# Re-spacing the key stage of a delta-rule block in a hand-interleaved decoder kernel

## The chip, the core and the metric

The kernel is one program on one core of one Trainium2 chip, written in Bass with the Tile framework. The metric is device microseconds of an execution, the median of three runs. All arithmetic is float32.

## What is computed

The reference is a decoder layer on a batch of 4 sequences of 512 tokens, width 512: a delta-rule attention (16 heads of 128 channels), then a quantised cross-attention, then softmax attention with a mixture of experts. The change touches only the first block:

```python
q = causal_conv(x @ Wq.T)   # 4 taps and silu; k and v alike
g = exp(-exp(A_log) * softplus(x @ Wa.T + dt_bias)); beta = sigmoid(x @ Wb.T)
q, k = l2norm(q), l2norm(k)                 # per head
for each token t:                           # state S: 128 x 128 per head
    error = v_t - g_t * (S^T k_t)
    S = g_t * S + k_t (beta_t * error)^T
    o_t = S^T q_t
out = (rmsnorm(o) * silu(x @ Wg.T)) @ Wo.T
```

## The kernel before, in words

**Pairs.** The recurrence is worked in chunks of 128 tokens, four per sequence. Work is cut into 32 pairs of heads (4 sequences times 8 pairs, `NP` = 32), and one pass of the main loop (line 993) handles pair m. Inside a chunk the recurrence becomes a triangular system whose inverse is needed for each of the pair's 8 head-chunks.

**Streams.** Each part is a Python generator that emits some instructions and yields. While `stage3(m)` (line 751, the recurrence itself, 15 yields) is emitted for pair m, the other streams are emitted between its yields. One round between two yields is called a turn here, T1 to T15. In a turn, in this order: one step of `output(m - 1)` (line 871, the product with Wo), two steps of `stage1(m + 2)` (line 552, keys and queries), one step of `stage2_values(m + 1)` (line 718, values and gates), and two steps of `inversions(m, turn)` (line 703).

**Who orders the engines.** The order on VectorE (DVE), ScalarE (ACT) and GpSimd (POOL) is the emission order, as line 977 asks. TensorE (PE) and the DMA queue of SyncE (SP) are not in that list: the framework's planner orders them from its own costs, so a PE instruction may be placed ahead of its place in the emission.

**stage1, in steps.** A `conv` (line 527) has four steps for keys and queries: half the projection (line 533), the other half with an ACT scaling (line 541), two of three DVE taps (line 544), the last tap with the silu (line 547). Steps 1 to 4 are the key of head 0, steps 5 to 8 that of head 1. Step 9 loads a table row (line 560) and the next weights, then turns the key of head 0 to tokens: four PE transposes (line 576), an ACT copy (line 578), four ACT squares that sum into `ss` (line 581). Step 10 does the same for head 1. Step 11 computes `rk`, `ee`, `ke`, `nr` from `ss` (lines 587 to 592: one on DVE, five on POOL) and scans the decay table `em` of head 0 on DVE (line 597), step 12 that of head 1. Steps 13 and 14, one per head, scale `em` by `ee` on ACT (line 402, four instructions), form key-by-key products on PE (line 606), combine both on DVE to `at` (line 609) and store it (line 610). Step 15 begins with `load_blocks` (line 668), which loads `at` back in the shape of the inversion (lines 672 and 673). Then follow the two query convs, the products (line 621), the decayed keys (line 402 again), and the sums of squares (line 652), to step 26. With two steps per turn, step 2k ends turn k.

**Inverses.** `stage2_inverse` (line 676) has 33 pieces: 31 elimination steps of two tensor operations each (lines 684 and 685), one with a copy and two stores (lines 690 to 692), one with the two loads (lines 697 and 698). Inverses of even pairs run on DVE, of odd pairs on POOL. In the pass of pair m, the inverse of m + 1 is finished and that of m + 2 begun, so a pass with even m finishes a POOL inverse while a pass with odd m finishes a DVE one. `inversions` takes one or two pieces per step, in turn; one turn is three pieces. The new inverse begins in the turn after next once `load_blocks` was emitted (`loaded > 4`), at one piece per step.

**stage3, by its yields.** Segments 1 to 4 join the inverse's quarters on PE and ACT (lines 765 to 799). Then, per chunk c: `r` (for c > 0: PE line 817, DVE line 819), `u` (PE line 826, ACT copy line 828), and the new state and outputs (PE lines 836, 844, 846; state on ACT line 839 or DVE line 841). Chunk 0 takes segments 5 and 6, chunk 1 segments 7 to 9, chunk 2 segments 10 to 12, chunk 3 segments 13 to 15.

**PSUM.** All of `pj`, `tp`, `pk`, `pw` and the like come from one pool of four buffers, `p_b` (line 342); the recurrence has its own.

**Start and end.** Before the loop, pairs 0 and 1 are prepared together with the cross-attention's keys and values (`prepare`, line 917, whose transposes of quantised keys are line 953). In the pass of pair 30 there is no `stage1`.

Of the kernel before, what the change touches and what calls it, by code (L numbers as in the profile page):

```python
# [31 lines left out]
F32 = mybir.dt.float32  # L32
AF = mybir.ActivationFunctionType
ALU = mybir.AluOpType
# [4 lines left out]
P = 128  # L39
B, S, D = 4, 512, 512  # L40
# [5 lines left out]
HG = 2  # L46
# [52 lines left out]
def decoder(ctx: ExitStack, tc: tile.TileContext, a: dict, out: bass.AP):  # L99
# [73 lines left out]
    def run(*gs):  # L173
        for g in gs:
            for _ in g:
                pass
# [154 lines left out]
    with ExitStack() as st:  # L331
# [64 lines left out]
        def chunks(t):  # L396
            return t.rearrange("p c j -> p (c j)")
# [121 lines left out]
        def load_weights(m, *what, by=nc.sync):  # L519

            for n in what:
                if m < B * NHG:
                    t = (s1 if n < 2 else s2).tile([P, KD, HG * P], F32, name=f"w{n}", bufs=1)
                    by.dma_start(t, a["a_w"][m % NHG][:, n])
                    weights[m, n] = t
# [26 lines left out]
        def stage1(m):  # L552

            b, hg = divmod(m, NHG)
            hh = slice(hg * HG, (hg + 1) * HG)
            wk, wq = weights.pop((m, 1)), weights.pop((m, 0))

            def rows(n):
                t = s1.tile([P, HG, S], F32, name=f"row{n}", bufs=1)
                nc.sync.dma_start(chunks(t), g_d[b, n, hg * HG * TB : (hg + 1) * HG * TB].rearrange("c t -> (c t)").partition_broadcast(P))  # L560
                return [t[:, p, :] for p in range(HG)]

            kT, kt = [], []
            ss = small.tile([P, HG * TB], F32, name="ss", bufs=2)
            for p in range(HG):
                t = live.tile([P, S], F32, name="kT")
                yield from conv(b, hg, p, 1, wk, t)
                kT.append(t)
                yield
            xnT, beta, gam, ngam, gend, gall = seqs[b]  # L570
            gb = rows(0)
            load_weights(m + 1, 1)
            for p in range(HG):
                tp = p_b.tile([P, TB, P], F32, name="pb")
                for c in range(TB):
                    nc.tensor.transpose(tp[:, c, :], kT[p][:, c * P : (c + 1) * P], ident)
                t = s1.tile([P, TB, P], F32, name="ktok")
                nc.scalar.copy(t, tp)
                kt.append(t)
                for c in range(TB):  # L580
                    nc.scalar.activation(tp[:, c, :], tp[:, c, :], AF.Square, accum_out=ss[:, p * TB + c : p * TB + c + 1])
                yield

            rk, ee, ke = (small.tile([P, HG * TB], F32, name=n, bufs=2) for n in ("rk", "ee", "ke"))
            nr = small.tile([P, HG * TB], F32, name="nr", bufs=4)
            flat = lambda t: t[:, hh, :].rearrange("p h c -> p (h c)")
            nc.vector.tensor_scalar(ss, ss, 1e-24, None, ALU.max)  # L587
            nc.gpsimd.tensor_tensor(rk, ss, mhalf[:, 0 : HG * TB], ALU.pow)  # L588
            nc.gpsimd.tensor_tensor(ee, rk, rk, ALU.mult)
            nc.gpsimd.tensor_tensor(ee, ee, flat(beta), ALU.mult)  # L590
            nc.gpsimd.tensor_tensor(ke, ee, flat(gend), ALU.mult)
            nc.gpsimd.tensor_tensor(nr, ss, rk, ALU.mult)
            em = []
            for p in range(HG):

                e = s1.tile([P, TB, P], F32, name="em")
                nc.vector.tensor_tensor_scan(chunks(e), gb[p], id4, 0.0, ALU.mult, ALU.add)
                em.append(e)
                yield
            ats = []  # L600
            for p in range(HG):
                scale(em[p], em[p], ee, p)
                pk = p_b.tile([P, TB, P], F32, name="pb")
                for c in range(TB):
                    k_ = kT[p][:, c * P : (c + 1) * P]
                    nc.tensor.matmul(pk[:, c, :], k_, k_, start=True, stop=True)
                at = live.tile([P, TB, P], F32, name="at", bufs=4)
                ats.append(at)
                nc.vector.scalar_tensor_tensor(at, pk, -1.0, em[p], ALU.mult, ALU.mult)
                nc.sync.dma_start(squares(at_d[m % SLOTS][p * TB : (p + 1) * TB]), at)  # L610
                yield
            load_blocks(m, ats)
            mb = rows(1)

            qh, qg, pt, sq, kd_ = [], [], [], [], []

            def product(p):
                pq = p_b.tile([P, TB, P], F32, name="pb")
                for c in range(TB):
                    cs = slice(c * P, (c + 1) * P)  # L620
                    nc.tensor.matmul(pq[:, c, :], kT[p][:, cs], qh[p][:, cs], start=True, stop=True)
                t = live.tile([P, TB, P], F32, name="pt", bufs=6)
                nc.vector.tensor_tensor(t, pq, em[p], ALU.mult)
                pt.append(t)

            def decayed(p):
                t = live.tile([P, TB, P], F32, name="kdec", bufs=4)
                scale(t, kt[p], ke, p)
                kd_.append(t)

            for p in range(HG):
                q = s1.tile([P, S], F32, name="qh")
                c = conv(b, hg, p, 0, wq, q)
                yield from itertools.islice(c, 2)
                if p:
                    product(0)
                yield from c
                qh.append(q)
                g = live.tile([P, S], F32, name="qg", bufs=6)
                nc.gpsimd.tensor_tensor(g, q, mb[p], ALU.mult)  # L640
                qg.append(g)
                t = w2.tile([P, S], F32, name="cv", bufs=5)
                nc.scalar.activation(t, q, AF.Square)
                sq.append(t)
                yield
            load_weights(m + 1, 0)
            decayed(0)
            yield

            pss = p_b.tile([P, S], F32, name="pb")  # L650
            for p in range(HG):
                nc.tensor.matmul(pss[p * 32 : (p + 1) * 32, :], tab_a[:, C_ONE, 0:32], sq[p], start=True, stop=True)
            sr = small.tile([P, S], F32, name="sr", bufs=1)
            nc.scalar.copy(sr[0 : 32 * HG], pss[0 : 32 * HG])

            rq = small.tile([P, HG * TB], F32, name="rq", bufs=2)
            for p in range(HG):
                nc.sync.dma_start(rq[p * P // HG : (p + 1) * P // HG, :], sr[p * 32 : p * 32 + 1, :].rearrange("o (n k) -> o n k", k=HG * TB))
            yield
            product(1)  # L660
            yield
            decayed(1)
            yield
            keys[m] = (kT, kd_, qg, pt, nr, rq)
# [38 lines left out]
        def inversions(m, turn):  # L703


            n, loaded, left = 0, 0, True
            while left or turn:

                for _ in range(1 + n % 2):
                    left = left and next(begun[m + 1], None) is not None  # L710
                n += 1
                loaded += m + 2 in inverses
                if turn and loaded > 4:
                    next(begun.setdefault(m + 2, stage2_inverse(m + 2)), None)
                yield
            begun.setdefault(m + 2, stage2_inverse(m + 2))
# [200 lines left out]
        def prepare():  # L917
# [24 lines left out]
            for kt in range(2):  # L942
                pk = p_b.tile([P, D], F32, name="pb")
                for kd in range(KD):
                    nc.tensor.matmul(pk, ctxT[kt][:, kd, :], wk[kd], start=kd == 0, stop=kd == KD - 1)
                k = temp()
                nc.vector.tensor_tensor(k, pk, bk, ALU.add)
                yield
                quantised(k, k, H2, HD2, small)
                yield  # L950
                tp = p_b.tile([P, KD, P], F32, name="pb")
                for kd in range(KD):
                    nc.tensor.transpose(tp[:, kd, :], k[:, kd * P : (kd + 1) * P], ident)
                t = temp()
                nc.scalar.copy(t, chunks(tp))
                yield
                nc.sync.dma_start(x_kT_d[:, :, kt * P : (kt + 1) * P], t.rearrange("p (c k) -> p c k", c=KD))
# [29 lines left out]
        pair0 = stage1(0)  # L987
        run(turns((start, 1), (itertools.islice(pair0, 2 * HG * 2), 1)))

        run(itertools.islice(pair0, 3 * HG + 1))  # L990
        run(turns((stage2_inverse(0), 2), (chain(pair0, turns((stage1(1), 2), (stage2_values(0), 1))), 1), (prepare(), 1)))
        begun[1] = stage2_inverse(1)
        for m in range(NP):
# [609 lines left out]
```

## Time and profile before

| what | us |
|---|---|
| median of 3 runs (3775.2 to 3777.73) | 3776.95 |
| the profiled execution | 3771.82 |
| its span, first to last instruction | 3769.0 |
| delta-rule passes in it (142 to 1962) | 1820.0, PE busy 1688.33 |
| its start (0 to 142) | 142.0, PE busy 95.87 |
| last pass and turn-over (1962 to 2150) | 188.0, PE busy 147.87 |
| the rest (2150 to 3769) | 1619.0, PE busy 1506.41 |
| PE granted clock, whole span | 0.961 |

A pass is told by the start of its first matmul of line 765. Busy times are unions of instruction times; matmul ends are modelled, so a gap between two rows is read from the bracket behind a timeline row (idle time before it, and what ended it), not from start plus duration. A float32 matmul of 512 columns is recorded as two instructions of 592 ns at full clock, so the half of a projection is a row "x4".

### The profile page before, as it was taken

The page shows a single profiled execution, that of the slowest core. Times are in us where ns is not written, and L with a number is a line of the kernel's source. Part 1 is how long each engine was busy: PE and PEld are TensorE (multiplying, and loading weights), DVE is VectorE, ACT ScalarE, POOL GpSimd, SP SyncE. Part 2 cuts the span into 40 slices and gives each one's busy share as a digit, 9 for nine tenths or more (in the row PEclk, how much of TensorE's full clock was granted, in tenths as well). Part 3 has the DMA queues.
Part 4 walks back from the last instruction along what each step waited for, and adds up shares of the span by engine and source line. Part 5 has one row for each costly group of instructions (what it writes and reads, how often), then busy time and mean ns, then how long its engine had stood idle before and what let it go on. Part 6 is the DMA issues. An engine that isn't in the chain of part 4 may idle for free. (4 is left out here: it accounts for less than half of the span.)

```text
span 3769.0 us, 48754 instructions
## 1 busy us (share of the span) xinstructions
PE 3438.5 (91%) x16466; PEld 1916.5 (51%) x16466; DVE 2208.8 (59%) x4923; ACT 1583.5 (42%) x4379; POOL 1378.5 (37%) x1941
## 2 busy tenths in 40 slices
PE   5889999999899999999997789999999999898897
PEld 3545555555555555555554455555555555554443
DVE  5667666775677666765674455656655655554111
ACT  3444444444444444444442243444544444343121
POOL 1544555346543564455543222213112111211442
PEclk7999999999999999999998799999999999999998
DMA  5334333433334342434341435445444544446444
GB/s 157 108 100 124 101 108 95 146 100 114 96 107 139 95 123 83 121 115 118 97 126 37 168 132 168 139 137 159 148 137 135 162 143 134 149 151 209 87 84 92
DMA packets 391879, 465.54 MB, mean 124 GB/s; under 512 B 128451, under 2 KB 242115, under 8 KB 391440
## 3 DMA queue, kind: packets, MB, share of 16 engines
q1 hardware_dynamic: 380080, 438.03, 37.7%
q0 software_dynamic: 10112, 21.58, 3.0%
q8 instruction: 131, 2.15, 0.2%
q10 hardware_dynamic: 1440, 2.84, 0.2%
q14 instruction: 116, 0.95, 0.1%
HBM read 401.76 MB, written 64.81 MB: 124 GB/s over the span
## 5 line engine op out<-in xcount | busy, mean ns | idle before, releaser
L533 PE MATMUL pb<-xnT,w 128*128 128x512 f32 x2048 | 974.5, 611 | 18.7 <-issue 9.9
L533 PEld LDWEIGHTS pb<-xnT,w 128*128 128x128 f32 x2048 | 374.4, 195 | 417.7 <-issue 399.8
L544 DVE SCALAR_TENSOR_TENSOR cv<-pb,pp,cv 128x510 f32<-128x510 f32 (+2 forms) x576 | 423.6, 744 | 29.9 <-ACT cv L541 17.6
L1145 PE MATMUL pb<-c_q,hT 128*128 128x512 f32 x768 | 358.2, 605 | 9.7 <-DMA c_q<-in_c_wq_dram 3.3
L685 POOL TENSOR_TENSOR iT<-iT,iW 32x31 f32<-32x31 f32 (+15 forms) x496 | 275.2, 555 | 38.9
L684 POOL TENSOR_TENSOR iW<-iA,iT 32x31 f32<-32x31 f32 (+15 forms) x496 | 249.1, 502 | 56.0 <-DMA iA<-at_d 13.7
L890 PE MATMUL pb<-wot,og 128*128 128x512 f32 x512 | 250.9, 613 | 2.0 <-issue 1.5
L1251 PE MATMUL pw<-c_o,oT 128*128 128x512 f32 x512 | 241.5, 602 | 2.9 <-DVE oT L1243 2.9
L1145 PEld LDWEIGHTS pb<-c_q,hT 128*128 128x128 f32 x768 | 142.7, 194 | 165.7 <-issue 152.8
L1217 ACT ACTIVATE e<-pb,nm,rq 128x128 f32<-128x128 f32 (+3 forms) x256 | 157.0, 618 | 143.8 <-DVE nm L1215 111.3
L685 DVE TENSOR_TENSOR iT<-iT,iW 32x31 f32<-32x31 f32 (+15 forms) x496 | 206.9, 417 | 17.1
L640 POOL TENSOR_TENSOR qg<-qh,row 128x512 f32<-128x512 f32 x64 | 82.6, 1291 | 358.7 <-ACT qh L547 311.2
L541 ACT ACTIVATE cv<-pb,pp 128x512 f32<-128x512 f32 x192 | 148.6, 774 | 153.4 <-PE pb L533 150.2
L684 DVE TENSOR_TENSOR iW<-iA,iT 32x31 f32<-32x31 f32 (+15 forms) x496 | 186.1, 375 | 45.8 <-DMA iA<-at_d 35.2
L895 DVE TENSOR_TENSOR xa<-pb,xa 128x512 f32<-128x512 f32 x112 | 76.9, 687 | 198.4 <-PE pb L890 198.4
L588 POOL TENSOR_TENSOR rk<-ss,mhalf 128x8 f32<-128x8 f32 x32 | 66.8, 2086 | 343.9 <-DVE ss L587 343.0
L279 POOL TENSOR_SCALAR x_e<-x_e 128x1024 f32<-128x1024 f32 x64 | 67.4, 1054 | 332.1 <-ACT x_e L274 235.5
L1241 PE MATMUL po<-eT,val 128*128 128x512 f32 x320 | 170.6, 626 | 6.9 <-ACT eT L1239 3.8
L274 ACT ACTIVATE x_e<-pb,nm 128x256 f32<-128x256 f32 x256 | 118.2, 476 | 111.7 <-DVE nm L271 105.8
L1211 PE MATMUL pb<-kT,qT 128*128 128x256 f32 (+3 forms) x576 | 162.7, 409 | 0.8 <-ACT x_e L274 0.8
L1073 POOL TENSOR_TENSOR rope_s<-q,tab 128x128 f32<-128x128 f32 x64 | 34.8, 544 | 315.8 <-DVE q L1175 269.9
L547 ACT ACTIVATE qh<-cv 128x512 f32<-128x512 f32 x64 | 40.3, 630 | 251.9 <-DVE cv L544 239.6
(330 smaller groups left out, 6596.1 us busy)
## 6 DMA issues: line engine op xcount, KB each, us to landing
c_o<-in_c_wo_dram SPq DMA_DIRECT2D x128, 512.0 KB, 4.0
c_q<-in_c_wq_dram SPq DMA_DIRECT2D x128, 512.0 KB, 4.6
w<-in_a_w_dram SPq DMA_DIRECT2D x124, 512.0 KB, 4.0
row<-g_d SPq DMA_DIRECT2D x64, 512.0 KB, 3.7
at_d<-at SPq DMA_DIRECT2D x64, 256.0 KB, 2.7
T<-t_d SPq DMA_DIRECT2D x32, 512.0 KB, 4.1
X<-x_d SPq DMA_DIRECT2D x32, 512.0 KB, 5.3
rrow<-r_d SPq DMA_DIRECT2D x32, 512.0 KB, 3.6
```

What stands on the lines that cost most here:

```text
L274: nc.scalar.activation(e[:, n, :], ps[r][:, g, :], AF.Exp, bias=nm[:, n : n + 1], accum_out=ssum[:, n : n + 1])
L533: nc.tensor.matmul(pj, wt[:, kd, p * P : (p + 1) * P], xnT[:, kd, :], start=kd == 0, stop=kd == KD - 1)
L541: nc.scalar.activation(ac, pj, AF.Identity, bias=cb[:, m, h : h + 1], scale=cw[:, m, h, 3:4])
L544: nc.vector.scalar_tensor_tensor(ac[:, j:], pj[:, : S - j], cw[:, m, h, 3 - j : 4 - j], ac[:, j:], ALU.mult, ALU.add)
L684: eng.tensor_tensor(u, A[:, i, i + 1 :].unsqueeze(2).to_broadcast([nb, n, w]), T[:, i, :w].unsqueeze(1).to_broadcast([nb, n, w]), ALU.mult)
L685: eng.tensor_tensor(T[:, i + 1 :, :w], T[:, i + 1 :, :w], u, ALU.add)
L890: nc.tensor.matmul(pw, og[p][:, c * P : (c + 1) * P], wot[:, p, :], start=p == 0, stop=p == HG - 1)
L1145: nc.tensor.matmul(pj, hT[:, kd, :], w[:, kd % 2, :], start=kd == 0, stop=kd == KD - 1)
L1211: nc.tensor.matmul(ps[:, m, k * P : (k + w) * P], qT[g][:, n + m, :], kT[:, g, j : j + w, :], start=True, stop=True)
L1217: nc.scalar.activation(e[n + m][:, :nk], ps[:, m, :nk], AF.Exp, bias=nm[:, n + m : n + m + 1], scale=rq, accum_out=es[:, n + m : n + m + 1])
L1241: nc.tensor.matmul(po, val[:, g, :], eT, start=k == 0, stop=k == c)
L1251: nc.tensor.matmul(pw, oT[:, h + m, :], w[:, m, :], start=g == 0 and h + m == 0, stop=g == 3 and h + m == 3)
```

## The change

In `stage1`, the key of head 0 is turned to tokens (and squared) inside the conv of head 1, after its second step (step 7), that of head 1 in step 10. The first `em` scan moves to step 9, the second to step 11. The table row is loaded at the start of `stage1`, except for pair 0. A step with nothing in it follows the second scan, and another lies between the two heads' scalings, so that these are steps 13 and 15, in turns T7 and T8; `load_blocks` and the first half of the query projection are step 16, and `stage1` ends with step 27. In `inversions`, one step in four takes two pieces, the others one (five pieces in two turns), and in the pass of pair 30 every step takes two. `prepare` yields once more between quantising a key tile and transposing it. No instruction is added or removed.

```diff
--- before.py
+++ after.py
@@ -560,17 +560,12 @@
                 nc.sync.dma_start(chunks(t), g_d[b, n, hg * HG * TB : (hg + 1) * HG * TB].rearrange("c t -> (c t)").partition_broadcast(P))
                 return [t[:, p, :] for p in range(HG)]
 
-            kT, kt = [], []
+            kT, kt, em, ats = [], [], [], []
             ss = small.tile([P, HG * TB], F32, name="ss", bufs=2)
-            for p in range(HG):
-                t = live.tile([P, S], F32, name="kT")
-                yield from conv(b, hg, p, 1, wk, t)
-                kT.append(t)
-                yield
-            xnT, beta, gam, ngam, gend, gall = seqs[b]
-            gb = rows(0)
-            load_weights(m + 1, 1)
-            for p in range(HG):
+            xnT, beta, gam, ngam, gend, gall = seqs[b] if m else seqs[b] + [None] * 5
+            gb = rows(0) if m else None
+
+            def by_token(p):
                 tp = p_b.tile([P, TB, P], F32, name="pb")
                 for c in range(TB):
                     nc.tensor.transpose(tp[:, c, :], kT[p][:, c * P : (c + 1) * P], ident)
@@ -579,7 +574,30 @@
                 kt.append(t)
                 for c in range(TB):
                     nc.scalar.activation(tp[:, c, :], tp[:, c, :], AF.Square, accum_out=ss[:, p * TB + c : p * TB + c + 1])
-                yield
+
+            def decays(p):
+
+                e = s1.tile([P, TB, P], F32, name="em")
+                nc.vector.tensor_tensor_scan(chunks(e), gb[p], id4, 0.0, ALU.mult, ALU.add)
+                em.append(e)
+
+            for p in range(HG):
+                t = live.tile([P, S], F32, name="kT")
+                c = conv(b, hg, p, 1, wk, t)
+                yield from itertools.islice(c, 2)
+                if p:
+                    by_token(0)
+                yield from c
+                kT.append(t)
+                yield
+            load_weights(m + 1, 1)
+            if m == 0:
+                xnT, beta, gam, ngam, gend, gall = seqs[b]
+                gb = rows(0)
+            decays(0)
+            yield
+            by_token(1)
+            yield
 
             rk, ee, ke = (small.tile([P, HG * TB], F32, name=n, bufs=2) for n in ("rk", "ee", "ke"))
             nr = small.tile([P, HG * TB], F32, name="nr", bufs=4)
@@ -590,14 +608,9 @@
             nc.gpsimd.tensor_tensor(ee, ee, flat(beta), ALU.mult)
             nc.gpsimd.tensor_tensor(ke, ee, flat(gend), ALU.mult)
             nc.gpsimd.tensor_tensor(nr, ss, rk, ALU.mult)
-            em = []
-            for p in range(HG):
-
-                e = s1.tile([P, TB, P], F32, name="em")
-                nc.vector.tensor_tensor_scan(chunks(e), gb[p], id4, 0.0, ALU.mult, ALU.add)
-                em.append(e)
-                yield
-            ats = []
+            decays(1)
+            yield
+            yield
             for p in range(HG):
                 scale(em[p], em[p], ee, p)
                 pk = p_b.tile([P, TB, P], F32, name="pb")
@@ -609,6 +622,8 @@
                 nc.vector.scalar_tensor_tensor(at, pk, -1.0, em[p], ALU.mult, ALU.mult)
                 nc.sync.dma_start(squares(at_d[m % SLOTS][p * TB : (p + 1) * TB]), at)
                 yield
+                if p == 0:
+                    yield
             load_blocks(m, ats)
             mb = rows(1)
 
@@ -706,7 +721,7 @@
             n, loaded, left = 0, 0, True
             while left or turn:
 
-                for _ in range(1 + n % 2):
+                for _ in range(1 + (n % 4 == 1 or m == NP - 2)):
                     left = left and next(begun[m + 1], None) is not None
                 n += 1
                 loaded += m + 2 in inverses
@@ -948,6 +963,7 @@
                 yield
                 quantised(k, k, H2, HD2, small)
                 yield
+                yield
                 tp = p_b.tile([P, KD, P], F32, name="pb")
                 for kd in range(KD):
                     nc.tensor.transpose(tp[:, kd, :], k[:, kd * P : (kd + 1) * P], ident)
@@ -987,7 +1003,7 @@
         pair0 = stage1(0)
         run(turns((start, 1), (itertools.islice(pair0, 2 * HG * 2), 1)))
 
-        run(itertools.islice(pair0, 3 * HG + 1))
+        run(itertools.islice(pair0, 8))
         run(turns((stage2_inverse(0), 2), (chain(pair0, turns((stage1(1), 2), (stage2_values(0), 1))), 1), (prepare(), 1)))
         begun[1] = stage2_inverse(1)
         for m in range(NP):
```

## The prediction

> **What bounds the kernel now.** I read the page first, then PE's waits over the delta-rule passes, then the timelines of one even and one odd pass, then the clock by windows.
>
> ```profile
> PE 3438.5 (91%) x16466; PEld 1916.5 (51%) x16466; DVE 2208.8 (59%) x4923; ACT 1583.5 (42%) x4379; POOL 1378.5 (37%) x1941
> ```
>
> PE is the bound, the others have slack, so only PE's idle time and its clock can be won. In the passes (142 to 1962) PE is busy 1688.33 of 1820.0 us: 131.7 us of idle in 30 passes. The view of PE's waits in that window says who ends it:
>
> ```profile
> PE pb L576 <- ACT kT L547: 38.2, 30, 2.3
> PE ps L836 <- ACT u L828: 23.3, 11, 2.6
> PE ps L826 <- DVE r L819: 14.5, 12, 1.4
> PE pb L533 <- issue: 9.9, 3, 3.3
> PE pb L621 <- ACT qh L547: 8.6, 7, 2.4
> PE ps L817 <- ACT state L839: 7.6, 26, 0.4
> ```
>
> (Columns: total us, times, longest.) The first is in every pass, nearly always 1.13 us. L836 and L621 stand in passes with even m, L826 in odd ones. Pass 14 (even), the timelines of all engines, shows how two of them arise:
>
> ```profile
> 1012.70 1.98 PE L890 MATMUL pb<-wot,og 128*128 128x512 f32 x4
> ...
> 1018.41 0.66 PE L576 MATMUL pb<-tab,kT 128*128 128x128 f32 x4 [1.13 <-ACT kT L547]
> 1023.72 1.43 POOL L684 TENSOR_TENSOR iW<-iA,iT 32x156 f32<-32x156 f32 x1
> 1023.69 2.54 DVE L597 TENSOR_TENSOR_SCAN em<-row,tab_a 128x512 f32<-128x512 f32 x2
> 1027.60 1.64 POOL L588 TENSOR_TENSOR rk<-ss,mhalf 128x8 f32<-128x8 f32 x1
> 1029.83 2.44 ACT L402 ACTIVATE em<-em,ee 128x128 f32<-128x128 f32 x8 [5.92 <-POOL ee L590]
> 1032.84 0.41 ACT L828 COPY u<-ps 128x128 f32<-128x128 f32 x2
> 1033.14 0.71 PE L836 MATMUL ps<-u,kdec 128*128 128x128 f32 x4 [2.37 <-ACT u L828]
> ```
>
> PE's 2.37 us are not the recurrence's own latency: its `u` copy stands on ACT behind eight scalings that wait 5.92 us for `ee`, which waits on POOL behind inverse pieces. In the odd pass 15, three pieces, both scans and three more pieces stand ahead of `r` on DVE (1081.57 to 1088.46), and line 826 waits 1.39 us. The clock, by windows:
>
> ```profile
> 1016.90:1020.30 3.40, 2.27 (x20) 1.85 (x19) 2.59 (x4) 2.52 (x7) 3.01 (x6) 1.00 0.00 0
> 1030.90:1034.30 3.40, 1.16 (x10) 1.16 (x11) 2.60 (x4) 3.02 (x9) 2.86 (x8) 1.00 0.50 113
> 1034.34:1037.75 3.41, 3.41 (x11) 2.18 (x10) 3.34 (x7) 0.33 (x1) 2.29 (x2) 0.50 1.04 255
> ```
>
> (PEclk is third from the end.) The 1.13 us gap leaves it at 1.00; the 2.37 us gap is followed by one 3.41 us window at 0.50.
>
> **The change, part by part.** No instruction comes or goes; all that moves is who stands behind whom.
>
> *Keys to tokens.* PE's position at the second key's transposes stays the same: between line 890's third product (1012.70) and line 576 at step 10 lie four transposes, 0.6 us, before and after, only in another place. The chain that ends the wait is unchanged too: DVE's add of that product, three taps at 744 ns, silu 0.63, ending 18.36 (times from 1000). So I book nothing for the largest wait. Its bounds: all 38.2 us, if the planner pulls a later projection in front; or a loss, costed as a rival. The copy and four squares of key 0 (0.60 + 4 x 0.40 = 2.2 us of ACT) now stand ahead of key 1's silu: transposes end near 15.1, ACT is through at 17.4, the taps end at 17.6. Hidden by 0.2 us; if not, those tenths go to the wait.
>
> *`ss` sooner, fewer pieces ahead of `ee`.* In T5 ACT turns one key, not two: `ss` is complete near 21.6, not 23.5, and the state copies behind it come 1.5 us earlier, which covers line 817's 0.4 us. Of the 7.6 us I take 6. In an even pass POOL is never idle here, so its queue decides: by T5 it has 13 pieces instead of 15, and the two that drop out (1023.72 to 1027.5) took 3.8 us with the scans beside them. `rk` can start near 23.6; `ee` comes at 26 to 26.8 instead of 29.8.
>
> *Scalings a turn apart.* Four scalings (1.22 us), not eight (2.44), stand ahead of `u`, so `u` is done near 29.2 instead of 33.1. PE with half the query projection (1.8 us) moved behind line 836 arrives there at about 27.8, with the whole of it placed ahead at 29.6. The wait thus becomes 0 to 1.4 us; I take 0.7. Three even passes show the same delay as `PE pb L533 <- issue` at 3.3 us, a projection waiting for the PSUM buffer that `at` frees. Together 33.2 us in 14 passes, less 14 x 0.7: 23.
>
> *Clock.* 13 half-rate windows follow these gaps and the 2.4 us gaps at line 621. At 3.41 us and half rate each costs up to 1.7: 22 us. The Trainium skill ("TensorE: Matmul & The Clock Gate", "Why this matters for your kernels") advises against PE gaps over about 3 us. By that rule only the three 3.3 us gaps cost clock, 5 windows, 8.5 us; by the rows, gaps of 1.9 to 2.6 us cost it often but not always. I go by the rows and take 15.
>
> *Odd passes.* From key 0's `vn` to `r`, DVE has one scan less (1.22 us, moved ahead of it) and one piece less, but most of its sum of 7.5 us stays in the queue: `r` comes 1 to 1.5 us sooner, while PE, with one `pk` (0.55 us net) moved to T8, arrives sooner as well. Of 14.5 I take 10. The skill ("GPSIMD Engine Reference", "1. Specifications") says that a DVE instruction with two SBUF inputs contends with GpSimd. The row agrees that the scan is one (1.43 us beside it against 0.48 for the piece before), and it speaks against this part: the first scan now runs beside `rq` and the pieces ahead of `ee`. By the rule alone both scans still delay `ee` by 0.9 us each, which is the 26.8 above; without it 26.
>
> *Queues on SP.* The table row's load moves to T1 (used in T5: free). The second `at` store and `load_blocks` move with step 15, half a turn later, but `at` itself is ready sooner (about 31 against 33), and the reload of the inverse, which stood just ahead of `iA` on SP, comes two turns later. It is used a pass later, with over 15 us to spare. `iA` should land before DVE's first piece of m + 2, which waited 1.72 us (pass 14) to 4.46 us (pass 18); the query taps stand behind it and line 621 behind those. Of 8.6 us I take 4, because SP's order is the planner's.
>
> *New waits.* In T9 the second query half is now followed closely by its taps: ACT 0.78, two taps 1.5, value tap 0.74, silu 0.63 = 3.7 us to the value transposes, with line 817 and the next half projection (0.5 + 1.8) to cover it. Bounds: 0, if the planner pulls the other half (1.8 us, same PSUM buffer), to 1.4 us a pass; nearest the row of pass 14, where two whole projections were placed ahead of line 729 without a wait. I take 0.3 x 29 = 9 us of loss. `stage1`'s 27th step puts 1.26 us of ACT scalings in T14, when ACT waits for DVE anyway (`gs` behind `og`): nothing. Slower pieces for even pairs on DVE (about 0.8 us each) shift load to T8: nothing booked.
>
> *Start and end.* PE waits 11.4 us in two gaps for the quantised keys (line 953). The extra yield puts a turn of other work there, but DVE, which makes them, stays as busy: 0 to 8, I take 3. At pair 31 (4.41 + 4.04 us for T and X) POOL runs without a break from before the pass to 1996; its pieces are the same, so emitting them faster changes nothing.
>
> *Sum:* 6 + 23 + 15 + 10 + 4 + 3 - 9 = 52 us. Against the profiled execution (3771.82, its span 3769.0) that is 3720; the median stood 5.1 us above it, and the forecast is against the median: 3776.95 - 52 = **3725**.
>
> **The rivals.**
> 1. *The key's turning is won as well* (8%): the planner puts work under the 1.13 us. For it: `tp` of key 0 frees its buffer near 17.4, one more free than before. Against it: the 30 waits in 30 passes come from a fixed chain. 3725 - 36 = 3689.
> 2. *The waits only change names* (9%): relief of `ee` is met by SP's order and the tight T9 chain at its full 1.4 us; half the clock and waits go, 52 - 32 = 20 us or less: 3757 to 3780.
> 3. *The keys hold ACT* (14%): the planner places key 0's transposes behind line 890's last product, so ACT's copy and squares start at 17.8, not 15.1, and both silus, the `u` copies and the second transposes stand behind them. The wait grows from 1.13 to about 3.4 us, 2.3 us in 30 passes (69 us), and at 2.4 us and over each may draw a half-rate window (up to 1.7). Less the 52 won: 3794, up to 3830 with the clock. It decides once ACT starts the squares later than about 15.3. Against it: a buffer is free at 13.6 and the transposes come next in the emission.
> 4. *The main case* (69%): 3690 to 3752.
>
> **How the numbers follow.** 0.2%, about 7.6 us, is what a measurement of this kernel can tell from no change. Faster: all of 4 and 1 and a third of rival 2, 0.80 less a little for a loss that I do not see: 0.78. Same: the middle of rival 2 and the good edge of 3, 0.08. Slower: 0.14. The range reaches from rival 1 to most of rival 2: 3675 to 3766, leaving the slower cases out.
>
> **What would show it.** Right: PE's wait at line 836 under 10 us in all, line 817's and the `issue` waits of line 533 gone, line 576's still near 38; ACT's wait for `ee` (129.8 us over the passes) shorter; the granted clock of the passes above 0.98; odd and even passes nearly equal, at about 57 us. Wrong: line 576's wait at 0 or at 3 us a pass; new waits at lines 729, 826 or 621 of over 1 us; or passes as long as before with other names in the view of waits.

## The result and the profile after

The changed kernel takes **3817.79 us** (median of 4 runs, 3812.59 to 3821.22) against 3776.07 us before on the same chip (4 runs, 3771.57 to 3777.73): a ratio of 1.0119, 95% interval 1.0102 to 1.0135. It is 42 us slower where 52 us were forecast to be won. The profiled span is 3815.5 us against 3769.0, and it comes apart so:

| stretch of the span | before | after | difference |
|---|---|---|---|
| start, to the first matmul of pass 0 | 142.7 | 151.2 | +8.4 |
| passes 0 to 29, even m (15 passes) | 912.9 | 954.4 | +41.5 |
| passes 0 to 29, odd m (15 passes) | 906.0 | 896.0 | -10.0 |
| pass 30 | 39.4 | 38.5 | -0.9 |
| pass 31 to the end | 1768.0 | 1775.4 | +7.4 |

In passes 0 to 29 PE is busy 1687.2 us before and 1692.1 us after, and idle 131.7 and 158.4 us. The trace's clock record has 81.9 us at half rate in these passes before, 119.5 us after. The two kinds of passes have to be read apart:

| passes 0 to 29 | PE idle before, after | PE busy before, after | half rate before, after |
|---|---|---|---|
| even m | 74.7, 99.6 | 838.2, 854.8 | 49.2, 88.2 |
| odd m | 56.8, 58.9 | 849.2, 837.1 | 32.5, 30.9 |

So the loss is in the even passes: PE stands, and its clock is lower afterwards. The gain of the odd passes is not idle time; it is taken up below.

The first part of the page, after:

```profile
PE 3453.7 (91%) x16466; PEld 1923.7 (50%) x16466; DVE 2184.3 (57%) x4923; ACT 1581.7 (41%) x4379; POOL 1378.1 (36%) x1941
```

It has the same counts as before, and only shows that no work was added. PE's waits over the passes (142 to 1990), the view that the prediction was built on:

```profile
PE ps L832 <- DVE state L856: 68.0, 38, 4.8
PE pb L571 <- ACT kT L547: 28.3, 30, 2.2
PE ps L841 <- DVE r L834: 11.5, 15, 0.8
...
PE ps L851 <- ACT u L843: 5.3, 15, 1.0
```

(Line 832 after is line 817 before, 571 is 576, 841 is 826, 851 is 836, 856 is 841.) The wait for `u` fell from 23.3 to 5.3 us and the `issue` waits of line 533 are gone, as forecast. But one wait that stood for 9.6 us in all before, for the recurrence's state, is now 68.0 us, up to 4.8 at a time. DVE's waits in the same window name what the state stands behind, first before, then after (line 684 before is line 699 after):

```profile
DVE iW L684 <- DMA iA<-at_d: 27.8, 10, 4.5
```

```profile
DVE iW L699 <- DMA iA<-at_d: 82.3, 14, 6.9
```

It now comes in 14 even passes, 4.8 to 6.9 us each. In pass 14 (even), DVE's timeline:

```profile
1064.23 0.69 DVE L746 TENSOR_TENSOR vn<-pb,nr 128x512 f32<-128x512 f32 x1 [0.82 <-PE pb L744]
1071.10 0.18 DVE L699 TENSOR_TENSOR iW<-iA,iT 32x31 f32<-32x31 f32 x1 [6.18 <-DMA iA<-at_d]
...
1072.53 1.51 DVE L544 SCALAR_TENSOR_TENSOR cv<-pb,pp,cv 128x511 f32<-128x511 f32 x2
...
1074.98 0.59 DVE L856 SCALAR_TENSOR_TENSOR state<-state,gall,ps 128x128 f32<-128x128 f32 x2
```

DVE stands 6.18 us ahead of the first piece of the inverse of m + 2; behind that piece are the query taps and, 3.9 us later, the state. PE's timeline in that pass has two gaps:

```profile
1045.79 0.66 PE L571 MATMUL pb<-tab,kT 128*128 128x128 f32 x4 [0.90 <-ACT kT L547]
...
1075.37 1.22 PE L832 MATMUL ps<-state,kT 128*128 128x128 f32 x4 [4.08 <-DVE state L856]
```

The key's gap is 0.90 us where it was 1.13. The second is new, and it draws a lower clock (windows of pass 14, PEclk third from the end):

```profile
1068.60:1072.00 3.40, 2.69 (x6) 0.54 (x5) 0.79 (x5) 0.00 (x0) 0.00 (x0) 1.00 0.92 241
1072.00:1075.40 3.40, 0.03 (x1) 0.03 (x1) 3.26 (x10) 0.00 (x0) 0.00 (x0) 0.68 0.38 151
1075.40:1078.70 3.30, 2.88 (x11) 2.36 (x12) 3.20 (x8) 2.34 (x7) 1.28 (x1) 0.50 0.02 5
1078.70:1082.10 3.40, 3.40 (x8) 1.16 (x9) 1.55 (x5) 1.14 (x3) 0.00 (x0) 0.80 0.41 154
```

The clock falls while PE is empty: the record has half rate from 1073.20, 1.9 us into the gap, to 1080.03, which is 6.83 us or two of the trace's steps of 3.41 us. Pass 14 before had one such step.

Why `iA` is late is on SP. From its timeline in pass 14, before, with rows left out at the dots:

```profile
1033.02 0.37 SPq L610 DMA_DIRECT2D at_d<-at  x1
1033.48 0.46 SPq L690 DMA_DIRECT2D t_d<-iT  x1
...
1038.38 0.38 SPq L697 DMA_DIRECT2D T<-t_d  x1
1038.86 0.52 SPq L673 DMA_DIRECT2D iA<-at_d  x1
```

and after:

```profile
1059.31 0.33 SPq L705 DMA_DIRECT2D t_d<-iT  x1
1059.73 0.52 SPq L623 DMA_DIRECT2D at_d<-at  x1
1061.35 0.31 SPq L707 DMA_DIRECT2D x_d<-iA  x1
1061.75 0.52 SPq L623 DMA_DIRECT2D at_d<-at  x1
1062.37 0.79 SPq L712 DMA_DIRECT2D T<-t_d  x1
1065.04 0.36 SPq L713 DMA_DIRECT2D X<-x_d  x1
1065.82 0.32 SPq L688 DMA_DIRECT2D iA<-at_d  x1
```

`at` of the second head was ready on DVE at 1057.83, but its store is issued at 1061.75, behind the store `x_d`, which waits for POOL's copy at the end of the other inverse (to 1061.32). `iA` reads what that store wrote, so it comes 4.1 us after the store, now behind both loads of the joined inverse. It takes 5.3 us to land beside them; before, with `T` alone ahead of it, it took 4.4. Counted from the start of pass 14, before against after: `at` ready 37.3 and 34.7, its store issued 37.3 and 38.6, `iA` issued 43.2 and 42.7, DVE at the piece 45.9 and 41.8. The change brought `at` 2.6 us and DVE 4.1 us forward, and left `iA` where it was: it lands 47.6 and 48.0 us into the pass.

The code explains the order. The stores `t_d`, `x_d` and the loads `T`, `X` are issued through `behind(SP)`, which ties them to the SP instruction that was emitted last. Before, when POOL's inverse reached its end, in T7, that was the second `at` store, so `t_d` could not pass it. After, that end is emitted in T8, after `load_blocks` and the load of the second table row (`rows(1)`): `t_d` is tied to this row load, which is ready early, and nothing holds it behind the `at` stores. SP is the planner's to order, and it put `t_d` first.

### The profile page after: what moved, and what is told of

It reads as the page before. It is cut to its first block, busy times and chain, and to the rows that moved or that the text cites. A ratio compares the mean times of both kernels' runs of the same rounds, so it can differ in the third digit from the quotient of the medians.

```text
span 3815.5 us, 48828 instructions
## 1 busy us (share of the span) xinstructions
PE 3453.7 (91%) x16466; PEld 1923.7 (50%) x16466; DVE 2184.3 (57%) x4923; ACT 1581.7 (41%) x4379; POOL 1378.1 (36%) x1941
## 5 line engine op out<-in xcount | busy, mean ns | idle before, releaser
L533 PE MATMUL pb<-xnT,w 128*128 128x512 f32 x2048 | 963.4, 604 | 3.7 <-DVE at L622 2.0
L541 ACT ACTIVATE cv<-pb,pp 128x512 f32<-128x512 f32 x192 | 149.1, 777 | 167.5 <-PE pb L533 165.9
L700 DVE TENSOR_TENSOR iT<-iT,iW 32x31 f32<-32x31 f32 (+15 forms) x496 | 195.0, 393 | 17.1
L402 ACT ACTIVATE em<-em,ee 128x128 f32<-128x128 f32 x256 | 81.9, 395 | 165.6 <-POOL ee L608 165.6
```

The costliest lines, as they stand in the source:

```text
L533: nc.tensor.matmul(pj, wt[:, kd, p * P : (p + 1) * P], xnT[:, kd, :], start=kd == 0, stop=kd == KD - 1)
L541: nc.scalar.activation(ac, pj, AF.Identity, bias=cb[:, m, h : h + 1], scale=cw[:, m, h, 3:4])
L700: eng.tensor_tensor(T[:, i + 1 :, :w], T[:, i + 1 :, :w], u, ALU.add)
```

## The experiments

**Theories.** S: the order on SP, as above, makes `iA` late; DVE stands in front of it and PE behind DVE. Its rivals: R, the query half that now comes close behind its taps makes the gap; P, the new pace of the inverse does; K, turning the keys sooner holds ACT; U, the `u` copies behind the scalings are still the limit. The texts below went on record before each run. Every kernel was timed beside the kernel before on the same chip; ratios are to that (its medians there were 3770.87 to 3776.51 us). "Even" and "odd" are mean lengths of passes 2 to 27 in the profiled execution, without 4, 5, 12, 13, 20 and 21, in which the next sequence is prepared; "half rate" is clock time in passes 0 to 29; "wait for `iA`" is DVE's.

| kernel | median us | ratio (95%) | start | even | odd | half rate | wait for `iA` |
|---|---|---|---|---|---|---|---|
| before | 3776.07 | 1 | 142.7 | 60.77 | 57.99 | 81.9 | 27.8 |
| after | 3817.79 | 1.0119 (1.0102 to 1.0135) | 151.2 | 63.24 | 56.55 | 119.5 | 82.3 |
| edge | 3727.40 | 0.9880 (0.9858 to 0.9902) | 149.1 | 57.22 | 56.62 | 34.1 | 0.0 |
| oldpace | 3850.14 | 1.0196 (1.0174 to 1.0219) | 152.7 | 65.92 | 56.14 | 139.9 | 51.9 |
| newpace | 3736.84 | 0.9906 (0.9884 to 0.9929) | 144.8 | 56.50 | 58.57 | 37.5 | 14.6 |
| keys | 3777.64 | 1.0010 (0.9997 to 1.0022) | 156.1 | 59.31 | 58.33 | 75.1 | 4.7 |
| space | 3844.57 | 1.0186 (1.0158 to 1.0215) | 147.9 | 65.93 | 57.27 | 126.3 | 50.6 |
| keys_pace | 3761.51 | 0.9969 (0.9958 to 0.9979) | 151.9 | 57.82 | 59.27 | 47.8 | 23.4 |
| pace_edge | 3725.67 | 0.9884 (0.9860 to 0.9908) | 147.3 | 56.29 | 58.31 | 44.4 | 0.8 |
| noprep | 3721.18 | 0.9874 (0.9849 to 0.9899) | 149.2 | 57.27 | 56.63 | 34.1 | 0.0 |
| space_edge | 3842.54 | 1.0186 (1.0166 to 1.0207) | 145.1 | 65.50 | 56.60 | 126.3 | 48.9 |
| space_pace_edge | 3720.27 | 0.9860 (0.9842 to 0.9878) | 145.1 | 58.40 | 56.10 | 41.0 | 0.0 |

The order of SP's instructions in an even pass, read from each program (`T` and `X` are the loads of the joined inverse, `w` loads of weights):

```
before             at  w  at  t_d x_d T   iA  X
after              t_d at x_d at  T   X   iA
edge, noprep       at  w  at  iA  t_d x_d T   w  X
oldpace            at  t_d x_d T  at  X   w   iA
newpace            at  t_d at x_d iA  T   X
keys               at  at  t_d x_d T  iA  X
space, space_edge  at  t_d x_d T  at  X   w   iA
keys_pace          t_d at  at  x_d iA T   X
pace_edge          at  w  at  iA  t_d x_d T   w  X
space_pace_edge    at  w  at  iA  t_d x_d T   w  X
```

**edge**: the changed kernel with two lines exchanged, so that the last SP instruction emitted ahead of the inverse's stores is the load of `iA`, the last of `load_blocks`.

```diff
-            load_blocks(m, ats)
             mb = rows(1)
+            load_blocks(m, ats)
```

> The changed kernel, with the two lines that load the new inverse's blocks and the second table row swapped, so that the planner may no longer place the old inverse's store (t_d) ahead of the iA load on SP. Theory S (SP's order: iA is issued behind t_d, x_d, T and X and lands 6 us after DVE needs it, DVE stands, and with it the state for line 832): the wait at line 832 falls from 68 us to under 15, even passes from 63.6 to about 57.5 us, the median from 3818 to 3720-3745. Rival R (the half-turn shift of the query steps leaves DVE too little time, whatever SP does): the wait stays above 55 us and the median at 3805-3825.

3727.4 us: 90 us less than after for one exchange that moves no work on PE, DVE, ACT or POOL in the emission. In the traces of passes 14 and 15 DVE, ACT and POOL run the same rows in the same order in both kernels, and PE does but for one place near line 667. SP's timeline in its pass 14:

```profile
1018.23 0.38 SPq L623 DMA_DIRECT2D at_d<-at  x1
1019.04 0.33 SPq L524 DMA_DIRECT2D w<-in_a_w_dram  x1
1020.39 0.37 SPq L623 DMA_DIRECT2D at_d<-at  x1
1024.15 0.32 SPq L688 DMA_DIRECT2D iA<-at_d  x1
1024.56 0.52 SPq L705 DMA_DIRECT2D t_d<-iT  x1
```

and, for the same stretch, DVE's first piece and PE's state product:

```profile
1027.37 0.69 DVE L699 TENSOR_TENSOR iW<-iA,iT 32x31 f32<-32x31 f32 x1
```

```profile
1033.16 0.75 PE L832 MATMUL ps<-state,kT 128*128 128x128 f32 x4 [0.32 <-DVE state L856]
```

The store goes out as `at` is ready (34.6 us into the pass, as after), `iA` is issued 4.3 us sooner than after, and DVE's piece stands with no bracket: there is no wait. The 4.08 us of PE are 0.32. PE's waits over the passes:

```profile
PE ps L832 <- DVE state L856: 23.2, 36, 1.0
```

Line 832 fell from 68.0 to 23.2 us, less far than S had asked (under 15): 0.7 to 1.0 us a pass remain with `iA` in time (newpace has 21.6 us there too), and what would shorten them was not tried. R, P and K leave all that they name in place in this kernel, so none of them makes the gap. Against after, PE in the passes is idle 53.8 us less (158.4 to 104.6) and busy 34.5 less (1692.1 to 1657.6); half rate with PE busy fell from 103.8 to 30.4 us, and half of that difference is 36.7.

**oldpace**: the changed kernel at the old pace of the inverse.

```diff
-                for _ in range(1 + (n % 4 == 1 or m == NP - 2)):
+                for _ in range(1 + n % 2):
```

> The changed kernel with the inverse's old pace (one or two pieces per step in turn). Theory S: SP still has t_d, x_d and T ahead of the second at store and X ahead of iA, and ee comes later again (two more pieces ahead of it), so it is no faster than the changed kernel: 3810-3850. Rival P (the slower pace is what costs): back to 3776 or below.

3850.14 us. If the new pace were the harm, this would have been faster. With more pieces per turn the inverse's end is emitted in T7 between the two `at` stores, and in SP's order all of `t_d`, `x_d`, `T` stand ahead of the second one; `iA` is issued 46.9 us into the pass. `ee` is late again too (35.0 against 30.5), and PE's wait for `u` is 63.2 us in all. P falls.

**newpace**: the kernel before with the new pace only (the same edit, reversed).

> The kernel before with the new pace alone. On SP t_d and x_d then stand around the second at store, but iA ahead of T and X. Theory S: a small effect, 3765-3795, with DVE's wait for iA in even passes 2 to 4 us as before. Rival P: most of the loss, above 3800.

3736.84 us, more than had been expected of it. `ee` comes 2.5 us sooner (31.2 against 33.7) and `u`'s wait falls from 23.3 to 1.0 us; `at` is sooner with it, and SP issues `iA` ahead of `T` and `X`. In pass 14 the piece that waits for it starts 2.9 us after its issue (1025.24 to 1028.14), where after, behind both loads, it took 5.3. Most of what was forecast for the whole change, about 35 of 52 us by the ratio, is in this one line. So U is right in part: `u` was a limit of the kernel before. But what freed it here is `ee` coming sooner, with the eight scalings still together.

**keys**: only the keys' part of the change (sooner transposes, the scans' places, the row load), without the empty step, at the old pace.

```diff
                 yield
-                if p == 0:
-                    yield
             load_blocks(m, ats)
```

(and the pace as in oldpace)

> The changed kernel's earlier turning of keys and its scans, with the scalings in one turn and the old pace. On SP both at stores are again ahead of t_d, and iA behind T as before the change. Theory S: odd passes shorter by about 1 us, even passes about as before, 3750-3780. Rival R has no half-turn shift here either and expects no loss; rival K (the squares of key 0 ahead of key 1's silu hold ACT) expects a longer wait at the key transposes, over 45 us, and 3790 or more.

3777.64 us, no change. Even passes gain 1.5 us, odd ones lose 0.3, the start is 13.4 us longer. PE's wait for the keys is 28.4 us against 40.5 over passes 0 to 29, all that ended it counted: the move itself does not hold ACT, and rival K falls for the passes.

**space**: the kernel before with only the empty step between the two scalings.

```diff
                 yield
+                if p == 0:
+                    yield
             load_blocks(m, ats)
```

(with one step more ahead of the loop, so that pair 0 stands at the same place)

> The kernel before with the empty step between the two heads' scalings alone (old pace, keys as before). SP's order in even passes is then at, t_d, x_d, T, at, X, w, iA. Theory S: iA is issued at 46 us or later in an even pass (43 before), even passes 64 us or more, median 3800-3850, slower than before although u stands behind four scalings only. Theory U (the delay of u behind the scalings is the bound, as the prediction had it): faster, 3735-3765.

3844.57 us. The slowdown of the whole change is in this part, and more: even passes 65.93, `iA` issued 47.2 us into the pass, DVE waiting 50.6 us for it. SP's order is that of oldpace. Its odd passes gain nevertheless, 57.27 against 57.99; why is told below, under the odd passes.

**keys_pace**: the changed kernel without the empty step, at the new pace.

> The changed kernel without the empty step between the scalings: earlier keys and new pace together. SP's order in even passes is t_d, at, at, x_d, iA, T, X. Theory S: iA at 38 to 41 us, DVE's wait for it under 2 us a pass, median 3720-3750. Theory R' (keys and pace together are what costs, SP's order or not): 3790 or more.

3761.51 us, short of what was expected. `iA` still waits behind both `t_d` and `x_d` (23.4 us for DVE), and a new wait came up for the queries' squares. From PE's waits over its passes:

```profile
PE pb L665 <- ACT cv L656: 17.3, 10, 2.6
```

Its odd passes are the longest of all (59.27). Against newpace the keys' part here loses, while in keys it was neutral: the parts do not add up.

**pace_edge**: the kernel before with the new pace and the exchange of edge.

> The kernel before with the new pace and with the two loads swapped, so that SP has at, w, at, iA, t_d, x_d, T. Theory S: iA at about 38 us, DVE's wait for it gone, even passes about 56 us, odd ones as with the new pace alone (58.5), median 3715-3737, no slower than the new pace alone (3737). If SP's order only matters together with the re-spacing, equal to 3737 within 4 us.

3725.67 us, within what was expected, but the passes say less: the wait for `iA` fell from 14.6 to 0.8 us, line 621's is gone too (0.0), and yet passes 0 to 29 take as long as in newpace (1772.6 us there, 1772.8 here). The 11 us between the medians do not come from the passes, and the intervals overlap. So a wait of DVE for `iA` of up to 3.3 us a pass cost PE nothing that can be measured here; waits of 4.8 to 6.9 us, as after, did.

**noprep**: edge without the extra yield in `prepare`.

```diff
                 quantised(k, k, H2, HD2, small)
                 yield
-                yield
```

> The changed kernel with the two loads swapped, and without the extra yield in prepare. The prediction's step (an extra turn hides the wait for the quantised keys) expects it slower by 3 us, 3727 to 3733; the traces, in which the start grew from 142.7 to 151.2 us with the same 11.5 us of wait, expect the start 0 to 6 us shorter, 3721 to 3727.

3721.18 us, start 149.2 against 149.1: that yield does nothing that can be measured. PE's two gaps for the quantised keys are 11.4 us before, 11.5 after.

**space_edge and space_pace_edge**: space with the exchange of edge, and the same with the new pace too. At the old pace the inverse's end is emitted ahead of the two exchanged lines, so SP's order is that of space; at the new pace `iA` moves to the front.

> The kernel before with the empty step between the scalings, and with the row load emitted ahead of load_blocks, at the old pace. In the program's order SP still issues iA last here, behind both loads of the joined inverse, as with the empty step alone. Theory S (the place of iA in SP's order decides): 3835 to 3855, as with the empty step alone, DVE's waits for iA 40 to 60 us. A rival (the exchange helps by itself, because the row load no longer stands between): under 3815.

> The kernel before with the empty step between the scalings, the new pace and the row load ahead of load_blocks; the keys are turned to tokens as before. SP issues iA ahead of t_d here. Theory S: no DVE wait for iA, even passes 56.2 to 57.2 us, and odd passes 56.3 to 57.0 as with the spacing; PE's wait for the keys stays near 40 us against 28; the start is some 3 us shorter than with the whole change: 3705 to 3730. The rival that all three parts of the change are needed together: 3740 or more.

3842.54 and 3720.27 us. Where the exchange leaves `iA` last it is worth nothing (space took 3844.57 us): what decides is the place of the `at` store and of `iA`, not the row load itself. The second is as fast as edge and noprep (the intervals overlap), so the keys' part is not needed; but its even passes, 58.40 us, missed the 56.2 to 57.2 that were expected. PE's waits over its passes show what came up instead:

```profile
PE pb L576 <- ACT kT L547: 38.2, 30, 2.3
PE ps L828 <- DVE r L821: 28.1, 26, 1.4
```

Line 828 (826 before) waits for `r` in even passes too now, about 0.96 us each, and the key's wait is the old one. Shorter odd passes (56.10 us) and a start of 145.1 us make up for it. The fastest of these versions, about 3720 us, beat the kernel before by 1.3 to 1.4%.

## Why the prediction was wrong

**The step that failed** is "Queues on SP": "`iA` should land before DVE's first piece of m + 2 [...] Of 8.6 us I take 4, because SP's order is the planner's." It gave two reasons. That `at` is ready sooner holds: 2.6 us in pass 14. That the reload of the inverse, "which stood just ahead of `iA` on SP, comes two turns later" does not: `T` is issued 39.3 us into pass 14, before it was 42.7, and now `X` stands ahead of `iA` too. Later in the emission is not later on SP. The prediction did not ask where the stores and loads of the other inverse would go once the slower pace moves their emission from T7 to T8, and the `at` stores half a turn later: their order on SP is only tied to the last SP instruction emitted, and the change replaced that one, the second `at` store, by a row load. The `at` store, ready at 34.7 us in pass 14, then stands 3.9 us behind `t_d` and `x_d`, `iA` waits for that store, and its landing behind `T` and `X` takes 5.3 us (4.4 before, 2.9 in newpace). So `iA` comes at the same time as before and all that DVE gained upstream, 4.1 us, is spent standing before it. edge shows it: one exchange, no wait for `iA`, 90 us. That the store's lateness and the landing beside the loads share the harm as these numbers say is read from the timelines; no run separates the two. keys_pace comes nearest: there the store is some 3.5 us late as well, but `iA` is ahead of both loads, and DVE waits at most 3.2 us a pass; that kernel differs in more than this.

**Its sign.** The relief was real but was paid back in one place. Before, the even passes' delay was spread over shorter waits (`u` 1.9 to 2.6 us, three `issue` waits of 3.3, line 621, line 817); after, it is one gap of 2.6 to 4.8 us at line 832, which costs clock as well. In pass 14, PE's idle time went from 3.90 to 5.84 us and the pass from 59.7 to 62.3.

**The other terms of the sum.**
- *Line 817: 6 us won.* Wrong. 9.6 became 68.0 us, and in edge, where `iA` is not late, still 23.2. The state copies on ACT did leave, but DVE's share of the state came to set this wait.
- *Scalings a turn apart: 23 us.* Right in size, not in its cause: 18.0 (`u`) and 9.9 (`issue`) us are gone. But newpace, with the scalings together, leaves only 1.0 us of `u` and nothing of `issue`. `ee` ends 3.2 us sooner in the pass (30.5 against 33.7); 3 to 3.8 were forecast. The new pace alone gives 2.5 us of it. The separation of the scalings, without the pace, gave nothing there (space: wait for `u` 30.7 us, with `iA` late).
- *Clock: 15 us.* Wrong here, as its gaps did not go: half rate 119.5 us, not less than 81.9. Going by the rows rather than by the rule that the prediction quotes was sound: in the passes before, each of the 13 gaps of 2.2 us and over was followed by half rate, and only 2 of the 10 between 1.5 and 2. With no gap over 1 us in its ordinary passes, edge has 34.1 us, all around passes 0, 5 and 13.
- *Odd passes: 10 us.* The sum is met, 10.0, by luck. Line 826's wait fell from 16.0 to 11.5 us, but line 832's rose, and PE's idle time in the odd passes did not fall (56.8 and 58.9 us). What fell is its busy time, by 12.1 us with as many matmuls and nearly the same half rate. Most of it is in the sums of squares (line 652, 667 after), one product of 32 columns for each head. From pass 15, before and then after:

```profile
1103.21 1.04 PE L652 MATMUL pb<-cv,tab_a 128*32 128x512 f32 x2
...
1105.24 1.05 PE L652 MATMUL pb<-cv,tab_a 128*32 128x512 f32 x2
```

```profile
1135.14 1.05 PE L667 MATMUL pb<-cv,tab_a 128*32 128x512 f32 x4
```

Before, half a projection stood between the two heads' products; after, they are neighbours and run side by side, and the time that this line keeps PE in the odd passes falls from 29.3 to 17.9 us. The traces have this in 12 odd passes of each of the seven kernels with the empty step and in no pass of the five without it, and the seven have the shorter odd passes (56.1 to 57.3 us against 58.0 to 59.3). No run separates it from what else the step moves. The prediction, which counted only idle time and clock, had no term for it.
- *Keys to tokens: nothing.* Nearly: the wait went from 1.13 to 0.90 us in most passes, 10 us in all. Rival 3, that the squares hold ACT, did not happen.
- *New waits in T9: 9 us of loss at line 729.* Line 744, its successor, is not in PE's list. The loss came later, at line 832.
- *Start: 3 us won.* Wrong: 8.4 lost. The extra yield is worth nothing (noprep). A wait in `prepare` for `at` grew from 1.5 to 5.4 us, and the six kernels with the keys' part begin their passes at 149.1 to 156.1 us, the six without it at 142.7 to 147.9. Which of its moves does it was not tried.

**The rivals.** Rival 2 had "relief of `ee` is met by SP's order" and the right place, but priced it as half the gain lost, 3757 to 3780; the case on the slower side was given to the keys alone. A wait for `iA` of about 6 us in nearly every even pass was not among the cases, and none of them reached 3818 by way of SP. The forecast's size is met by edge (3727.4 against 3725), though not by its terms: there the clock and the `issue` waits paid more, the state and the start less than nothing.

**Its signs.** Of what was to show it right, line 836's wait under 10 us and the vanished `issue` waits came true while the kernel got slower; ACT's wait for `ee` rose from 129.8 to 155.6 us, although `ee` is sooner in the even passes, as ACT comes there sooner still; the passes' clock above 0.98 and even passes near 57 us failed (0.97 and 63.2), and these two told the truth, as did line 817's wait, which was to go and grew.

## What to carry to other kernels

When a change moves work in time, list for each in-order queue what its instructions wait for, and who is queued behind each of those, in the new order: an early store behind a late one is as late as that one. Where an order is tied to "the last instruction emitted", moving any emission moves the tie. Relief upstream counts only if each later input of the same engine comes sooner as well; the time at which that input is issued, counted from the start of the pass, is the row to compare. And a sum that comes out as forecast is no proof of its terms: compare idle and busy time for each kind of pass.

## What the runs showed of the hardware

- A gap of 4.1 us on PE came with 6.8 us of half rate (pass 14 after), the 2.37 us gap before with 3.4, and gaps up to 1 us with none (edge's ordinary passes have a granted clock of 1.00). In the passes before and after, every gap of 2.2 us and over had half rate begin in it or within 5 us behind it. Length is not all: a gap of 3.3 us in pass 21 of edge had none, and in its pass 5 a stretch of 6.8 us at half rate begins at 448.7 with no gap over 0.15 us in the 13 us ahead of it.
- Two products of 32 columns, for different rows of the output, took 1.05 us side by side, and 1.04 and 1.05 us one at a time (lines 667 and 652 in pass 15).
- The same load of 128 KB, `iA`, was there 2.9 us after its issue with `T` and `X` behind it (newpace), 4.4 us with `T` in front (before) and 5.3 us with both in front (after), each in pass 14.
- From pass 31 on the program is the same, with 6838 recorded matmuls in both, yet it took 1768.0 us before and 1775.4 after: PE is busy 1620.8 and 1628.0 us, with 160.3 and 177.9 us at half rate. Other kernels here lie between 1803 and 1817 us from pass 30 on, more with more half rate. What sets it was not found; differences of 7 us in the whole can come from there.
